# Scores in column groups and block transposes in the first layer of a two-layer attention kernel

## The chip, the core and the metric

The kernel runs on one core of a Trainium2 chip. A core has four compute engines with instruction streams of their own: TensorE (PE in the profile; its weight loads are shown as PEld), VectorE (DVE), ScalarE (ACT) and GpSimd (POOL). A fifth, SyncE (SP), issues most of the transfers. Each engine works through its stream in order, and the engines wait for each other by semaphores. The metric is the time of one execution on the device in microseconds; lower is better.

## The reference

The input x has 8 batches of 1024 tokens (64 positions l times 16 positions f) with 128 channels, in float32. The first layer is attention with 8 heads of width 128, whose scores are normalised twice, then a feed-forward layer with 512 hidden units and two layer norms:

```python
scores = jnp.einsum('bhlfc,bhmgc->bhlfmg', q, k) / jnp.sqrt(jnp.float32(c))
a = jax.nn.softmax(scores, axis=4)
a = jax.nn.softmax(a, axis=5)
z = jnp.einsum('bhlfmg,bhmgc->bhlfc', a, v)
...
z1 = _layer_norm(attn_out + x, ln1_g, ln1_b)
ffy = jax.nn.relu(z1 @ w1.T + b1) @ w2.T + b2
return _layer_norm(ffy + z1, ln2_g, ln2_b)
```

For one query, the 1024 scores are a grid of 64 positions m by 16 positions g. The first softmax runs over m, so it needs 16 sums of 64 exponentials each; the second runs over g, 64 sums of 16.

The second layer is additive attention within a batch, followed by a recurrence over the tokens with a sigmoid:

```python
scores = jnp.einsum('d,bijd->bij', v, jnp.tanh(Wi[:, None, :, :] + Wi[:, :, None, :]))
attn = jax.nn.softmax(scores, axis=-1)
C = jnp.einsum('bij,bjd->bid', attn, B)
```

That is a tanh for every pair of tokens and every channel. The scores are symmetric, so the kernel computes about half of the pairs.

## The kernel before

A program that runs when the data are within bounds (`fast_path`) does the work; a second, general program stands behind a branch and isn't entered here. The lines named below are those of the kernel before.

**First layer (`layer0`, once for each batch b).** The transposed input xT (channels on partitions, 1024 tokens along a row) is loaded by SP. For each head, `project` (L903) makes the query side u, with the product of the key and query weights folded into one matrix A, and `values` (L917) makes the values with the output weights folded in. For each of the 8 tiles of 128 queries:

- `scores` (L939): two products of 128 queries by 512 keys into the PSUM tile sc, so that a partition holds one query with all of its 1024 keys.
- the exponential on ACT, in place in PSUM (L942).
- `first_sums` (L946, DVE): 16 sums of 64; `first_inverse` (L949): 16 reciprocals; `divide` (L952): sc times these, into a half of the SBUF tile e.
- after two such tiles, a pair: one exponential over 2048 columns (L963, ACT), `second_sums` (L966) and `second_inverse` (L969) on DVE, and for each half `divide_again` on POOL (L980).
- the attention weights then have to stand with keys on partitions: for each half, eight transposes of 128x128 on PE (L853), four to a PSUM bank, and two copies of 128x512 out of PSUM into aT (L865 on DVE; for the first batch also L863 on ACT).
- `attend` (L994): eight products of 128x256, summed over the key tiles, and `gather` (L999 for head 0, L1001 else, DVE), which adds the result to zs.

After the heads follow the norm, the feed-forward part (`hidden`, `relu`, `outer`), which keeps its hidden units in an aT buffer, and the second norm.

**Second layer (`layer1`).** For each group of rows of the pair grid (`group`), either ACT computes tanh row by row with a bias (L1107), or POOL (L1117) or DVE (L1111, and a few L1117) adds the rows first and one wide tanh on ACT (L1165) follows. The rows stand in parts of a large SBUF tile th, which are given out and taken back (`Room`, `Span`). `times_v` (L1185) multiplies the rows by v on PE. Each of its products has 32 output partitions and uses one of four column groups of the array, into sa; a set of four fills all 128 partitions. After all rows of a tile come an exponential (L1281) and the attention of the second layer (L1314). At the end of the program, with all batches done, comes the recurrence (L1497, L1499).

**What sets the order.** All of this isn't issued as written. Every operation is registered with a `Plan` (`add`): the engines that it may run on and a cost in microseconds for each, the keys that it reads and writes, a priority and, if it needs one, a PSUM bank or a part of th. `Plan.emit` is a list scheduler: it keeps a clock for each engine, takes the engine that can start first and, among the operations that can start within 0.15 us of that, the one with the lowest priority number, and issues it. The tanh rows have several engines to choose from and go to the one that is free first in this reckoning. So a change of one operation's cost moves rows between ACT, POOL and DVE all through the program. PE operations have a mode, "full" or "groups" (column groups); a change of mode costs 0.1 us in the reckoning, and staying in the mode is preferred a little. The reckoning's costs are fixed numbers in the source; what the chip takes is another matter.

The first layer of batch b+1 runs beside the second layer of batch b (`pace` sets the priorities). The first layer of batch 0 runs with little beside it, and the second layer of batch 7 has nothing beside it at the end. `through_bank` registers a PE operation that takes one of the banks m0, m1 (for the first part of batch 0 also the two halves of sa) and the operation that empties it.

SBUF buffers that matter: two e pairs in `wx` (`es`, NE = 2), two aT buffers, th with 20 N columns (N = 1024). For batch 0 the values of the eight heads stand in th from 12 N on.

Of the kernel before, what the change touches and what calls it, by code (L numbers as in the profile page):

```python
# [10 lines left out]
AF = mybir.ActivationFunctionType  # L11
# [622 lines left out]
def fast_path(ctx: ExitStack, tc: tile.TileContext, a: dict, fits):  # L634
# [16 lines left out]
    NE = 2  # L651
# [33 lines left out]
    room = 20 * N  # L685
# [4 lines left out]
    aTs = ring("aT", 2, [P, NT, 2 * P])  # L690
    es = [wx[:, 4 + 2 * i : 6 + 2 * i, :] for i in range(NE)]
# [51 lines left out]


# [92 lines left out]
    count = {"aT": 0}  # L837

    def next_aT():
        count["aT"] += 1  # L840
        return (count["aT"] - 1) % 2

    def through_bank(pe, weight, r, evict, where, more, w, pri, choice=two):

        bank = Bank(*choice)
        n = len(plan.ops)
        add(("PE", weight), lambda _: pe(bank()), r=r, w=[("bank", n)], pri=pri, take=bank, wait=more + w)
        add(where, lambda e: evict(e, bank()), r=[("bank", n)] + more, w=w, pri=pri, give=bank)
# [23 lines left out]
    def layer0(b):  # L872
        alone = b == 0
        STRETCH = 0.95 if b < NB - 1 else 1.25
        xT, kx = xTs[b % 2], ("xT", b % 2)
        kz = ("zs",)
# [12 lines left out]
        for n_part, part in enumerate(parts):  # L889
# [3 lines left out]
            for h in range(H):  # L893
# [3 lines left out]
                if alone:  # L897
                    vp, kvp = th[:, (12 + h) * N : (13 + h) * N].rearrange("p (t c) -> p t c", c=C), ("vp0", h)
                for s in range(2) if part is None else (part,):
                    cols = slice(s * 512, (s + 1) * 512)  # L900

                    def project(bank, h=h, cols=cols):
                        nc.tensor.matmul(bank, A[:, h, :], xT[:, cols], start=True, stop=True)  # L903
# [20 lines left out]
                for qt in qts:  # L924
# [3 lines left out]
                    pair, q = (b * H * NT + i) // 2 % NE, qt % 2  # L928
# [3 lines left out]
                    r1, r2 = st[:, q, 0:G], st[:, :, G : G + M]  # L932
                    sc3 = sc.rearrange("p (m g) -> p m g", g=G)
                    e3 = e.rearrange("p (m g) -> p m g", g=G)

                    def scores(_, sc=sc, u=u, qt=qt):
                        for s in range(2):
                            cols = slice(s * 512, (s + 1) * 512)
                            nc.tensor.matmul(sc[:, cols], u[:, qt * P : (qt + 1) * P], xT[:, cols], start=True, stop=True)  # L939

                    add(("PE", 1.74), scores, r=[kx, ("u", h % 2, qt // 4)], w=[kc], pri=L0)
                    add(("ACT", 0.98), lambda _, sc=sc: nc.scalar.activation(sc, sc, AF.Exp, scale=SCALE),  # L942
                        r=[kc], w=[kc], pri=L0)

                    def first_sums(_, sc=sc, r1=r1):
# [642 lines left out]
```

## Time and profile before

| | us |
|---|---|
| median of 3 runs (5319.22 to 5320.98) | 5320.47 |
| the profiled execution | 5316.93 |
| its span, first to last instruction | 5315.0 |
| mean granted TensorE clock in it | 0.993 |

The profile gives for each engine the time in which it was busy, and for each group of instructions the busy time, the mean duration of one and the idle time of the engine in front of them with what ended it. The busy share by slices of a fortieth of the span, in tenths:

```profile
PE   8899999999999999999999999999999999986567
PEld 6555555555555555555555455555555455542125
DVE  7899999999999999999999999999999999988885
ACT  5489999999999999999999999999999999999994
POOL 2365779899998999999998999999899999987991
```

Three stages can be seen: the first three slices, some 400 us, in which the first layer of batch 0 runs and ACT is half idle; a long even part; and the last five slices, in which only the second layer of batch 7 and the recurrence are left. Most of the tanh work is in these groups:

```profile
L1117 POOL TENSOR_TENSOR th<-wiT 128x1024 f32<-128x1024 f32 (+59 forms) x2303 | 3345.5, 1487 | 215.2 <-PE sa L1185 196.0
L1165 ACT ACTIVATE th<-th 128x2634 f32<-128x2634 f32 (+53 forms) x997 | 2734.8, 2774 | 9.3 <-DVE th L1117 6.0
L1185 PE MATMUL sa<-th,vpat 128*32 128x512 f32 (+36 forms) x24576 | 2009.0, 459 | 202.2 <-ACT th L1165 186.9
L1111 DVE TENSOR_SCALAR_CACHE_REDUCE th<-wiT 128x344 f32<-128x344 f32 (+59 forms) x1930 | 1602.9, 867 | 68.6 <-PE sa L1185 65.8
L1107 ACT ACTIVATE th<-wiT 128x512 f32<-128x512 f32 (+62 forms) x1904 | 1369.8, 793 | 11.8 <-PE sa L1185 11.8
```

A line reads: source line, engine, operation, output and input tiles, form, count; then busy time in us and mean duration of one in ns; then the idle time before the group. A float32 product of PE appears as two records, so 24576 are 12288 products; a transpose is one record. ACT's tanh, 2734.8 and 1369.8 us, is more than three quarters of its time.

### The profile page before, as it was taken

Reading aid. Unit: us, or ns where it says so; the run is one execution under the profiler, and the core shown is the slowest. Engines: PE = TensorE matmul, PEld = TensorE weight load, DVE = VectorE, ACT = ScalarE, POOL = GpSimd, SP = SyncE. Lnnn points to the kernel's source line nnn. Section 1 sums busy time; section 2 is a strip of 40 time slices with the busy share of each in tenths; the row PEclk is TensorE's granted clock in tenths of the full one; section 3 lists DMA queues with packets and bytes.
Section 4 is the critical chain, followed back from the end, with each engine's and each line's share of the span. In section 5 each row is a group of like instructions: output and inputs, shape, how many; then the busy total and the mean of one; then the engine's idle time right before and its main releaser. Section 6 shows DMA issues by size and latency. Waiting matters only on the chain.

```text
span 5315.0 us, 98773 instructions
## 1 busy us (share of the span) xinstructions
PE 5007.1 (94%) x39173; PEld 2763.8 (52%) x39173; DVE 4884.6 (92%) x8676; ACT 5057.1 (95%) x4042; POOL 4522.8 (85%) x3113
## 2 busy tenths in 40 slices
PE   8899999999999999999999999999999999986567
PEld 6555555555555555555555455555555455542125
DVE  7899999999999999999999999999999999988885
ACT  5489999999999999999999999999999999999994
POOL 2365779899998999999998999999899999987991
PEclk9999999999999999999999999999999999999999
DMA  2000000000000000000000000000000000000001
GB/s 62 1 5 1 1 1 5 1 9 1 1 5 7 3 1 5 5 5 1 1 5 5 5 1 1 5 6 4 1 1 3 7 1 1 1 29 9 1 1 69
DMA packets 27335, 37.68 MB, mean 7 GB/s; under 512 B 2512, under 2 KB 19280, under 8 KB 26864
## 3 DMA queue, kind: packets, MB, share of 16 engines
q1 hardware_dynamic: 24832, 27.99, 1.6%
q8 instruction: 310, 5.08, 0.4%
q10 hardware_dynamic: 1872, 3.16, 0.2%
q14 instruction: 161, 1.32, 0.1%
q0 software_dynamic: 160, 0.13, 0.0%
HBM read 19.22 MB, written 12.06 MB: 6 GB/s over the span
## 4 chain that ended last, share of the span: by engine, by line
PE 67%; ACT 16%; DVE 10%; issue 6%; POOL 1%; DMA 0%; ACTq 0%; DVEq 0%; SPq 0%; POOLq 0%
PE sa L1185 25%; PE m L994 13%; PE sc L939 13%; ACT th L1165 9%; PE m L853 8%; ACT th L1107 4%; DVE th L1111 2%; PE m L1314 2%; PE m L917 2%; DVE stat_e L966 2%; PE m L903 1%; DVE stat_e L946 1%; ACT wx L963 1%; ACT sc L942 1%; DVE aT L865 1%
## 5 line engine op out<-in xcount | busy, mean ns | idle before, releaser
L1117 POOL TENSOR_TENSOR th<-wiT 128x1024 f32<-128x1024 f32 (+59 forms) x2303 | 3345.5, 1487 | 215.2 <-PE sa L1185 196.0
L1165 ACT ACTIVATE th<-th 128x2634 f32<-128x2634 f32 (+53 forms) x997 | 2734.8, 2774 | 9.3 <-DVE th L1117 6.0
L1185 PE MATMUL sa<-th,vpat 128*32 128x512 f32 (+36 forms) x24576 | 2009.0, 459 | 202.2 <-ACT th L1165 186.9
L1111 DVE TENSOR_SCALAR_CACHE_REDUCE th<-wiT 128x344 f32<-128x344 f32 (+59 forms) x1930 | 1602.9, 867 | 68.6 <-PE sa L1185 65.8
L1107 ACT ACTIVATE th<-wiT 128x512 f32<-128x512 f32 (+62 forms) x1904 | 1369.8, 793 | 11.8 <-PE sa L1185 11.8
L1185 PEld LDWEIGHTS sa<-th,vpat 128*32 128x32 f32 x24576 | 652.2, 110 | 1319.1 <-issue 842.2
L980 POOL TENSOR_TENSOR wx<-wx,stat_e 128x1024 f32<-128x1024 f32 x512 | 981.6, 1938 | 398.9 <-DVE stat_e L969 213.7
L939 PE MATMUL sc<-xT,wx 128*128 128x512 f32 x2048 | 983.5, 605 | 13.1 <-DVE wx L952 11.9
L994 PE MATMUL m<-aT,wx 128*128 128x256 f32 x3584 | 824.6, 384 | 7.2 <-DVE aT L865 7.2
L994 PEld LDWEIGHTS m<-aT,wx 128*128 128x128 f32 x3584 | 673.5, 191 | 187.8 <-issue 51.9
L865 DVE COPY aT<-m 128x512 f32<-128x512 f32 x940 | 616.6, 684 | 67.6 <-PE m L853 64.3
L946 DVE TENSOR_REDUCE stat_e<-sc 128x16 f32<-128x1024 f32 x512 | 613.5, 1204 | 38.9 <-ACT sc L942 37.7
L966 DVE TENSOR_REDUCE stat_e<-wx 128x128 f32<-128x2048 f32 x256 | 583.6, 2280 | 52.5 <-ACT wx L963 51.9
L952 DVE TENSOR_TENSOR wx<-sc,stat_e 128x1024 f32<-128x1024 f32 x512 | 619.9, 1214 | 3.2
L853 PEld LDWEIGHTS m<-ident,wx 128*128 128x128 f32 x3968 | 445.2, 141 | 309.4 <-issue 168.8
L942 ACT ACTIVATE sc<-sc 128x1024 f32<-128x1024 f32 x512 | 515.2, 1010 | 69.0 <-PE sc L939 52.8
L853 PE MATMUL m<-ident,wx 128*128 128x128 f32 x3968 | 558.6, 278 | 12.5 <-DVE aT L865 6.9
L939 PEld LDWEIGHTS sc<-xT,wx 128*128 128x128 f32 x2048 | 355.4, 191 | 385.8 <-issue 334.3
L963 ACT ACTIVATE wx<-wx 128x2048 f32<-128x2048 f32 x256 | 487.6, 1905 | 15.7 <-DVE wx L952 15.6
L969 DVE RECIPROCAL stat_e<-stat_e 128x128 f32<-128x128 f32 x256 | 240.9, 941 | 0.1
L1111 DVE DVE_READ_ACCUMULATOR th<-wiT 128x1 f32 x1930 | 160.8, 83 | 0.0
L917 PEld LDWEIGHTS m<-Wvo,xT 128*128 128x128 f32 x1080 | 133.9, 193 | 51.2 <-issue 25.0
(182 smaller groups left out, 2835.5 us busy)
## 6 DMA issues: line engine op xcount, KB each, us to landing
xT<-in_xt_dram SPq DMA_DIRECT2D x8, 512.0 KB, 3.6
th<-in_x_dram SPq DMA_DIRECT2D x8, 512.0 KB, 6.8
parked<-X SPq DMA_DIRECT2D x16, 256.0 KB, 2.3
xr<-parked SPq DMA_DIRECT2D x8, 512.0 KB, 8.1
parked_wx<-bT SPq DMA_DIRECT2D x14, 256.0 KB, 2.0
wx<-parked_wx SPq DMA_DIRECT2D x7, 512.0 KB, 3.2
out_dram<-ot ACTq DMA_DIRECT2D x8, 256.0 KB, 3.2
out_dram<-ot SPq DMA_DIRECT2D x8, 256.0 KB, 3.2
```

The source lines that it names most:

```text
L853: nc.tensor.transpose(bank[:, i * P : (i + 1) * P], s, ident)
L865: nc.vector.tensor_copy(dst, src)
L939: nc.tensor.matmul(sc[:, cols], u[:, qt * P : (qt + 1) * P], xT[:, cols], start=True, stop=True)
L946: nc.vector.tensor_reduce(r1, sc.rearrange("p (m g) -> p g m", g=G), AX.X, ALU.add)
L966: nc.vector.tensor_reduce(r2, e2.rearrange("p q (m g) -> p q m g", g=G), AX.X, ALU.add)
L980: nc.gpsimd.tensor_tensor(e3, e3, r2[:, q, :].unsqueeze(2).to_broadcast([P, M, G]), ALU.mult)
L994: nc.tensor.matmul(bank()[:, :256], vp[:, t, :], aT[:, t, :], start=t == 0, stop=t == NT - 1)
L1107: nc.scalar.activation(rows(c)[:, r, :], wiT[:, i0 + begin[c] :], AF.Tanh, bias=w_i(c, r))
L1111: nc.vector.tensor_scalar(rows(c)[:, r, :], wiT[:, i0 + begin[c] :], w_i(c, r), 0.0, ALU.add, ALU.add, accum_out=next_unused())
L1117: eng.tensor_tensor(rows(c), wiT[:, i0 + begin[c] :].unsqueeze(1).to_broadcast(shape), w_i(c).unsqueeze(2).to_broadcast(shape), ALU.add,)
L1165: nc.scalar.activation(slot()[:, a:z], slot()[:, a:z], AF.Tanh)
L1185: nc.tensor.matmul(sa[32 * c : 32 * c + 32, s:s1], vpat[:, 31 - r0 - r : 63 - r0 - r], rows(c)[:, r, s - at0 - begin[c] : s1 - at0 - begin ...
```

## The change

Layer 0's tiles of scores are laid out in another way, so that the block transpose of VectorE, which transposes 32x32 blocks, can take the place of the transposes on PE.

- xT holds the tokens in another order: the host puts token number 256 a + 32 b + r (a of 4, b of 8, r of 32) into column 128 b + 32 a + r, where before it stood in column 256 a + 32 b + r. `tokens` is the view of xT with the quarter a in front.
- `scores`: for a tile of 128 queries, 16 products instead of two. For each block s of 32 queries and each quarter a of the keys, the 32 queries are the stationary operand and the 256 keys of the quarter stream; the result goes to partitions 32 a to 32 a + 31, columns 256 s to 256 s + 255. A partition now holds one query's scores for a quarter of the keys, for each of four queries.
- `first_sums` gives 64 numbers for a partition (four queries by 16) that are sums over a quarter of the keys only. `totals`, four products of 32x64 on PE with the constant `same_row`, add the four quarters up and put the totals on all four partition groups, in a PSUM bank. `first_inverse` takes 64 reciprocals from the bank, and `divide` works as before on the new layout.
- After `divide_again`, `nc.vector.transpose` turns e in place, block by block of 32x32 (one instruction of 128x1024 for each half), in place of eight transposes on PE and two copies. `attend` streams the columns of e in runs of 32.
- The aT buffers are gone. There are three e pairs instead of two (NE = 3), handed out in turn, and the feed-forward part keeps its hidden units in an e pair. th grows by 448 columns. For batch 0 the values of heads 6 and 7 stand in buffers of X and B.
- `by_pe` is False throughout, so its branch isn't built. The costs given to the planner: totals 0.15, first_inverse 0.5 (before 0.2), the block transpose 1.17; the scores keep 1.74, in mode "groups".

```diff
-    NE = 2
+    NE = 3
...
-    room = 20 * N
+    room = 20*N+448
...
-    aTs = ring("aT", 2, [P, NT, 2 * P])
-    es = [wx[:, 4 + 2 * i : 6 + 2 * i, :] for i in range(NE)]
+    es = [wx[:, 4 + 2 * i : 6 + 2 * i, :] for i in range(2)] + ring("e", NE - 2, [P, 2, N])
...
+    same_row = tile_of(const, "same_row", [P, 32])
+    nc.vector.tensor_reduce(same_row, ident.rearrange("p (a r) -> p r a", a=4), AX.X, ALU.add)
...
+        tokens = xT.rearrange("p (b a r) -> p a b r", a=4, r=32)
...
-                    vp, kvp = th[:, (12 + h) * N : (13 + h) * N].rearrange("p (t c) -> p t c", c=C), ("vp0", h)
+                    at = 12 * N + h % 6 * N
+                    vp, kvp = th[:, at : at + N].rearrange("p (t c) -> p t c", c=C), ("vp0", h)
+                    if h >= 6:
+                        vp, kvp = (Xs[1], ("X", 1)) if h == 6 else (Bs[1][:, :, 0:C], ("B", 1))
...
-                        for s in range(2):
-                            cols = slice(s * 512, (s + 1) * 512)
-                            nc.tensor.matmul(sc[:, cols], u[:, qt * P : (qt + 1) * P], xT[:, cols], start=True, stop=True)
...
+                        for s in range(4):
+                            rows = slice(qt * P + 32 * s, qt * P + 32 * s + 32)
+                            for a in range(4):
+                                nc.tensor.matmul(
+                                    sc[32 * a : 32 * a + 32, 256 * s : 256 * s + 256], u[:, rows],
+                                    tokens[:, a], start=True, stop=True,
+                                )
...
+                        def first_sums(_, sc=sc, quarter=quarter):
+                            nc.vector.tensor_reduce(
+                                quarter.rearrange("p (s g) -> p s g", s=4),
+                                sc.rearrange("p (s m g) -> p s g m", s=4, g=G), AX.X, ALU.add,
+                            )
+
+                        def totals(bank, quarter=quarter):
+                            for a in range(4):
+                                nc.tensor.matmul(
+                                    bank[32 * a : 32 * a + 32, 0 : 4 * G], same_row, quarter, start=True, stop=True
+                                )
+
+                        def first_inverse(_, bank, quarter=quarter):
+                            nc.vector.reciprocal(quarter, bank[:, 0 : 4 * G])
+
+                        def divide(_, e=e, sc=sc, quarter=quarter):
+                            r = quarter.rearrange("p (s g) -> p s g", s=4).unsqueeze(2).to_broadcast([P, 4, G, G])
+                            nc.vector.tensor_tensor(quarters(e), quarters(sc), r, ALU.mult)
+
+                        add(("DVE", 1.15), first_sums, r=[kc], w=[k1], pri=L0)
+                        through_bank(totals, 0.15, [k1], first_inverse, ("DVE", 0.5), [], [k1], L0, banks, "groups")
+                        add(("DVE", 1.22), divide, r=[kc, k1], w=[ke], pri=L0)
...
-                        for s in range(2):
-                            through_bank(
-                                transposes([e[:, t * P : (t + 1) * P] for t in range(4 * s, 4 * s + 4)]), 0.52, [ke],
-                                copy(aT[:, 4 * s : 4 * s + 4, q * P : (q + 1) * P]), evict(0.68), [],
-                                [("aT", na, q, s)], L0, banks,
-                            )
+                        add(("DVE", 1.17), lambda _, e=e: nc.vector.transpose(e, e), r=[ke], w=[ke], pri=L0)
...
+                    keys = e2.rearrange("p q (s b r) -> p b (q s) r", s=4, r=32)
...
-                            nc.tensor.matmul(bank()[:, :256], vp[:, t, :], aT[:, t, :], start=t == 0, stop=t == NT - 1)
+                            nc.tensor.matmul(bank()[:, :256], vp[:, t, :], keys[:, t], start=t == 0, stop=t == NT - 1)
...
-        "xt": np.asarray(x).reshape(NB, N, C).transpose(0, 2, 1),
+        "xt": np.asarray(x).reshape(NB, 4, 8, 32, C).transpose(0, 4, 2, 1, 3).reshape(NB, C, N),
```

## The prediction

> **What bounds the kernel now.** I read the busy shares first, then the chain of waits, then four stretches cut at the ends of the 64th, 128th and last scores exponential (L942 at 392, 876 and 4687 us; a batch has 64 query tiles).
>
> ```profile
> PE 5007.1 (94%) x39173; PEld 2763.8 (52%) x39173; DVE 4884.6 (92%) x8676; ACT 5057.1 (95%) x4042; POOL 4522.8 (85%) x3113
> ...
> PE 67%; ACT 16%; DVE 10%; issue 6%; POOL 1%; DMA 0%; ACTq 0%; DVEq 0%; SPq 0%; POOLq 0%
> ...
> 0.00:392.00 392.00, 359.19 (x1729) 241.81 (x1730) 331.40 (x464) 241.72 (x372) 167.06 (x107) 1.00 0.08 22
> 392.00:876.00 484.00, 475.29 (x3379) 274.68 (x3377) 454.20 (x673) 470.03 (x540) 352.26 (x221) 1.00 0.01 2
> 876.00:4687.00 3811.00, 3749.47 (x29840) 2052.09 (x29838) 3593.12 (x6312) 3784.75 (x2746) 3554.17 (x2463) 1.00 0.01 4
> 4687.00:5315.00 628.00, 423.13 (x4231) 195.18 (x4229) 505.92 (x1229) 560.62 (x387) 449.33 (x324) 0.96 0.06 22
> ```
>
> Columns of the last four: length, then PE, weight loads, DVE, ACT, POOL. The chain says PE, 67%. But in the third stretch, 72% of the span, ACT is busy 3784.75 of 3811 us (99.3%): 26 us idle. PE is at 98.4%, DVE 94.3%. Two engines are full at once, so relieving PE alone can return no more there than ACT's 26 us plus whatever ACT work goes. In the first stretch ACT has 150 us idle and PE and DVE set the pace; in the last, PE has slack and ACT is full until the recurrence.
>
> The rows that the change touches:
>
> ```profile
> L952 DVE TENSOR_TENSOR wx<-sc,stat_e 128x1024 f32<-128x1024 f32 x512 | 619.9, 1214 | 3.2
> L865 DVE COPY aT<-m 128x512 f32<-128x512 f32 x940 | 616.6, 684 | 67.6 <-PE m L853 64.3
> L946 DVE TENSOR_REDUCE stat_e<-sc 128x16 f32<-128x1024 f32 x512 | 613.5, 1204 | 38.9 <-ACT sc L942 37.7
> ...
> L853 PE MATMUL m<-ident,wx 128*128 128x128 f32 x3968 | 558.6, 278 | 12.5 <-DVE aT L865 6.9 <-POOL wx L980 1.8 <-ACT aT L863 1.4
> ...
> L969 DVE RECIPROCAL stat_e<-stat_e 128x128 f32<-128x128 f32 x256 | 240.9, 941 | 0.1
> ...
> L949 DVE RECIPROCAL stat_e<-stat_e 128x16 f32<-128x16 f32 x512 | 117.8, 236 | 0.5
> ```
>
> **The change on PE.** Removed: 8 transposes for each of 512 tiles, 4096 at 558.6/3968 = 0.141 us: -577 us. The scores become 16 products of 32x256 instead of 2 of 128x512. The tanh products already run in this form:
>
> ```profile
> 3206.04 1.94 PE L1185 MATMUL sa<-th,vpat 128*32 128x256 f32 x32
> 3207.92 1.99 PE L939 MATMUL sc<-xT,wx 128*128 128x512 f32 x4
> 3209.74 1.04 PE L853 MATMUL m<-ident,wx 128*128 128x128 f32 x8
> ...
> 3118.93 1.10 PE L1185 MATMUL sa<-th,vpat 128*32 128x64 f32 x64
> 3119.96 1.12 PE L903 MATMUL m<-xT,A 128*128 128x512 f32 x2
> ```
>
> A matmul is two records, so the first line is exactly 16 products of 32x256: 1.88 us from start to start, against 1.82 for a tile's scores now (1.72 elsewhere). I take +0.11 x 512 = +56. The fourth line is 32 products of 64 columns in 1.03 us, 0.032 each; four for the totals are 0.13, x 512 = +66. PE: 5007 - 577 + 56 + 66 = 4552, 86%. That scores and attention now stream columns in runs of 32 is shown by no row; between 0 and 6% (a strided L946 against a dense L966: 1204 for 1024 against 2280 for 2048) of their 1925 us, 0 to +115. I take 0; PE is not the bound either way.
>
> L994 followed by L1185 takes 3.55 us from start to start (517.58 to 521.13), followed by full-size work 3.46 (255.99 to 259.45): 0.09 for a change of form, which lies inside the 1.88 above. Counted in the two instruction orders, changes between full size and column groups fall from 1730 to 1352, since the scores now stand beside the tanh products. [...]
>
> **DVE, per tile.** Two copies of 512 go (616.6/940 = 0.656 each). A 128x1024 block transpose comes; no row shows one. From below: the slope of L865, (684 - 281)/384 = 1.05 ns a column between 512 and 128 columns, gives 1.07; from above L1111 at 1024 columns, 1.27. I take 1.21, L952's, which is as wide. [...] The reciprocal grows from 16 to 64 columns: 0.236 + 48 x (0.941 - 0.236)/112 = 0.54, so +0.31 on 117.8/512 = 0.23; bounds 0 and +0.71. The sums keep their 1024 inputs and L946's price, the division L952's: 0 for both (if 64 outputs for 16 cost, L966 with 128 outputs says no).
>
> **What the planner moves.** The tanh rows go to whichever engine its list scheduler finds free, so the two instruction orders must be counted, stretch by stretch. Prices: an L1111 row with its accumulator read 0.29 + 1.037 us per 1000 columns (1272 + 83 at 1024, 490 + 83 at 270); L1107 0.216 + 0.838 and L1165 0.154 + 0.838 (slope from 3612 at 4096 and 1856 at 2000, the rest from their sums 1369.8 and 2734.8); an ACT copy of L863 0.57; an L1117 on DVE 101.7/80 = 1.27.
>
> To the 64th exponential, DVE: 58 copies fewer -38, 60 transposes +73, 63 reciprocals +20, 24 rows and 7474 columns more +15, one L1117 +1: +70, 401 us. ACT: 62 copies fewer -35, L1107 +116 rows, 25950 columns +47, L1165 +8, 21256 columns +19: 273.
> To the 128th, DVE: 119 copies -78, 64 transposes +77, reciprocals +20, 20 rows and 24083 columns +31, seven L1117 +9, norms -3: 510. ACT: -154 rows, -14961 columns -46; +32, +89134 columns +80; copies -3: 501.
> To the 512th, DVE: 772 copies -506, 386 transposes +467, 384 reciprocals +119, 98 rows and 90730 columns fewer -123, sixteen L1117 fewer -20, norms +3: 3533. ACT: +27261 columns of L1107 +23; -45 and -151606 of L1165 -134: 3674. POOL 69 fewer of L1117: about 3454.
> After it: ACT +5, DVE 0.
>
> So early work grows and the long stretch loses 111 us of ACT work, mostly the same work done sooner. Stretch one, cut again at 60 us: 60 us of start (DVE 27 busy), then 374 us of DVE, which ran at 305/332 = 92% with PE (308) at 93% beside it; PE now has room, so 96.5%: 388, in all 448 (+56). Two: 510 at 97%: 526 (+42). Three: ACT 3674 at 99.5%: 3692 (-119); DVE then stands at 95.7%. Four: 633 (+5). Sum 5299, against the span of 5315.0. The profiled run took 5316.93, 1.9 more than its span, and the median is 3.5 above it: forecast 5304, own range 5287 to 5320.
>
> What hides what: the round trip DVE to PE to DVE for the totals is hidden by other DVE work standing between sums and reciprocal (never fewer than one instruction in the new order, mostly two to six). Behind a late reciprocal DVE's in-order queue stops; next late are the division, ACT's second exponential and POOL's L980, which waits for L969 already (213.7 us). The new wait for a bank takes the place of four bank fills per pair. The third e pair and the other placing of the first batch's values add no instruction; a spare buffer can save a wait, 0 taken. The block order of xT is the host's; its eight loads keep their 512 KB, their queue and place.
>
> **Rivals.**
> 1. The round trip is not hidden, and DVE becomes the bound. DVE waits 0.07 us a copy for PE now (64.3/940), and 0.16 a gather (39.9 us on 256 gathers, L999 and L1001). At 0.16 a totals product, with its other waits kept: stretch one 60 + 374 + 27 + 10 = 471; two 510 + 30 + 10 = 550; three 3533 + 218 - 64 + 61 = 3748; four 633: 5402, and 5407 as a median. It decides once DVE's share of the third stretch stays under 95.3% (3533/3708, the length that brings the sum back to 5315). For it: in none of the four stretches does DVE pass 94.3%. Against: its waits were on a PE at 98%.
> 2. An exchange: idle times stay, the early loss cancels the gain: 462 + 525 + 3700 + 633 = 5320, median 5325: no change. For it: ACT was full before. Against: idle in stretch one came while PE was full.
> 3. PE was the true bound, as the chain says: every stretch closes to its fullest engine at 99% (60 + 374/0.99 = 438; 510/0.99 = 515; ACT 3674/0.999 = 3677; the last 633 less 8 = 625): 5255, median 5260. Against: ACT's 26 us.
> That the scores in column groups do not overlap is excluded by the 3206.04 line.
>
> **How the numbers follow.** Forecast 0.42, rival 1 0.30, rival 2 0.15, rival 3 0.13. A measurement of this kernel tells about 0.2%, 11 us, from no change. Faster: most of the forecast and rival 3, 0.46; within: rival 2 and the forecast's upper edge, 0.16; slower: rival 1 and the rest, 0.38. The range, 5250 to 5395, reaches past rival 3 and nearly to rival 1; the transpose at 1.07 (-72 us of DVE) and at 1.27 (+31) lie in it.
>
> **What would show it.** PE near 86%; scores near 1.9 us a tile; transposes near 1.21; reciprocals near 0.54; the 64th exponential at about 448, the 128th at 974, the last at 4666; ACT over 99% between the last two. Wrong if DVE waits for the totals by more than 0.1 us a tile, if a transpose takes 1.4, or if ACT's idle time between the last two passes 45 us.

## The result, and the profile after

| | before | after |
|---|---|---|
| median, us (4 runs each, same chip) | 5319.88 | 5369.98 |
| lowest to highest | 5319.22 to 5320.98 | 5367.01 to 5372.08 |
| span of the profiled execution | 5315.0 | 5364.7 |
| mean granted TensorE clock | 0.993 | 0.974 |

The ratio is 1.0093, with a 95% interval of 1.0077 to 1.0109: the changed kernel is 50 us slower. The forecast was 5304, 16 us faster.

The busy times and the chain of waits of the changed kernel, from its page:

```profile
PE 4753.6 (89%) x53509; PEld 2598.9 (48%) x53509; DVE 4941.9 (92%) x8132; ACT 5017.7 (94%) x3947; POOL 4578.8 (85%) x3162
...
ACT 40%; PE 34%; DVE 15%; issue 9%; POOL 1%; DMA 0%; ACTq 0%; SPq 0%; DVEq 0%; POOLq 0%
```

PE did get 253 us lighter and the chain left it (67% before, 34% now). ACT has 39 us less to do than before. What grew is the time in which ACT does nothing: 5315.0 - 5057.1 = 258 us before, 5364.7 - 5017.7 = 347 us now. That account, ACT's busy time plus its idle time, is used below; it doesn't say what causes the idle time.

The same kernel cut at the 64th, 128th and 512th scores exponential. Columns: length, then PE, weight loads, DVE, ACT and POOL busy, the granted clock, DMA share and rate:

```profile
0.00:473.60 473.60, 381.40 (x3919) 237.67 (x3920) 398.24 (x520) 274.04 (x436) 192.23 (x127) 0.93 0.07 19
473.60:1001.80 528.20, 486.61 (x5643) 269.46 (x5645) 506.36 (x673) 511.45 (x419) 475.25 (x315) 0.98 0.01 2
1001.80:4734.90 3733.10, 3458.51 (x39772) 1899.36 (x39766) 3529.13 (x5701) 3669.62 (x2700) 3439.24 (x2388) 0.99 0.01 4
4734.90:5364.70 629.80, 427.09 (x4197) 192.43 (x4185) 508.17 (x1241) 562.61 (x396) 472.03 (x334) 0.94 0.06 21
```

Beside the forecast (the cuts of the kernel before, at its exact markers, are 392.8, 884.1 and 4690.2):

| stretch | before | forecast | after | ACT busy, forecast / after | DVE busy, forecast / after |
|---|---|---|---|---|---|
| 1 | 392.8 | 448 | 473.6 | 273 / 274.0 | 401 / 398.2 |
| 2 | 491.3 | 526 | 528.2 | 501 / 511.5 | 510 / 506.4 |
| 3 | 3806.1 | 3692 | 3733.1 | 3674 / 3669.6 | 3533 / 3529.1 |
| 4 | 624.8 | 633 | 629.8 | 566 / 562.6 | 506 / 508.2 |

The work on ACT and DVE was forecast within about 2% in each stretch. Two lengths miss: the first by 26 us, the third by 41. In both, ACT waits longer than the forecast allowed.

The waits of ACT, after and then before: engine, line, what it waited for, us in total, times, longest.

```profile
ACT sc L956 <- PE sc L948: 131.6, 50, 10.8
ACT wx L1024 <- DVE wx L1013: 61.1, 12, 28.8
```

```profile
ACT sc L942 <- PE sc L939: 52.8, 49, 6.3
...
ACT wx L963 <- DVE wx L952: 15.6, 12, 3.4
```

The first exponential waits for scores (+79 us), the second for the division (+45 us). And DVE itself, did it wait for the totals? The groups of the changed kernel that answer to the forecast's prices:

```profile
L1042 DVE STREAM_TRANSPOSE wx<-wx 128x1024 f32<-128x1024 f32 x342 | 416.7, 1225 | 3.9 <-POOL wx L1039 3.8
...
L1009 DVE RECIPROCAL stat_e<-m 128x64 f32<-128x64 f32 x492 | 261.7, 534 | 22.1 <-PE m L1004 20.9
...
L1004 PE MATMUL m<-stat_e,same_row 128*32 128x64 f32 x3936 | 149.5, 226 | 57.7 <-DVE stat_e L997 43.5 <-DVE stat_e L1009 4.9 <-DVE wx L867 2.2
```

It hardly did: 20.9 us over the program, 0.04 us a tile. The delay is there all the same, and is seen when each reciprocal is paired with the sums it belongs to in the timeline:

| mean, us | before, stretch 1 / 2 / 3 | after | totals left out (`no_totals`, below) |
|---|---|---|---|
| end of the sums to start of the reciprocal | 0.9 / 1.2 / 1.4 | 3.3 / 4.5 / 6.3 | 1.5 / 1.6 / 1.5 |
| start of the sums to end of the division | 4.7 / 5.2 / 5.5 | 7.6 / 8.8 / 10.6 | 6.1 / 6.4 / 6.9 |

DVE fills the gap with other work, as forecast; but the tile's scores stay in sc until the division has read them, and there are two sc tiles. In stretch one a tile now holds its sc for about 2.0 us of products, 1.0 of exponential and 7.6 up to the end of the division, 10.6 us, or 5.3 us a tile with two of them, out of (473.6 - 60)/64 = 6.5. Before it was 1.9 + 1.0 + 4.7, or 3.8 of 5.2. The waits that lie between add to both.

Where it is worst can be seen in one place. ACT around 1060 us (start, length, and in brackets the idle time in front):

```profile
1042.39 1.01 ACT L956 ACTIVATE sc<-sc 128x1024 f32<-128x1024 f32 x1 [8.80 <-PE sc L948]
...
1046.43 1.01 ACT L956 ACTIVATE sc<-sc 128x1024 f32<-128x1024 f32 x1
1076.23 1.91 ACT L1024 ACTIVATE wx<-wx 128x2048 f32<-128x2048 f32 x1 [28.79 <-DVE wx L1013]
...
1089.38 5.30 ACT L1164 ACTIVATE th<-wiT 128x1024 f32<-128x1024 f32 x5 [8.37 <-DVE wiT L1289]
```

From 1033.6 to 1089.4, 56 us, ACT is idle for 46 in these three waits, and has no tanh row in its stream. The kernel before has only one wait above 3 us in all of its third stretch (3.81). The longest of the three is traced here; that the other two come of the totals as well isn't shown. DVE and then PE in the same place:

```profile
1050.86 1.16 DVE L997 TENSOR_REDUCE stat_e<-sc 128x64 f32<-128x1024 f32 x1
...
1052.59 1.21 DVE L997 TENSOR_REDUCE stat_e<-sc 128x64 f32<-128x1024 f32 x1
...
1072.67 0.55 DVE L1009 RECIPROCAL stat_e<-m 128x64 f32<-128x64 f32 x1
```

```profile
1058.57 2.08 PE L1098 MATMUL m<-zs,w_sb 128*128 128x512 f32 x2
...
1066.44 1.06 PE L1120 MATMUL m<-w_sb,wx 128*128 128x128 f32 x8
1067.34 3.62 PE L1050 MATMUL m<-e,wx 128*128 128x256 f32 x16
1071.53 0.32 PE L1004 MATMUL m<-stat_e,same_row 128*32 128x64 f32 x8 [0.58 <-DVE zs L1056]
```

The sums of the two tiles are done at 1052.0 and 1053.8; the first totals, 0.3 us of work, run at 1071.5. In PE's in-order stream they stand behind the feed-forward part of the batch (L1098, L1120) and an `attend` (L1050), which take the same two banks and themselves wait for DVE. Both sc tiles wait for totals, so no new scores come. Before, sums, reciprocal and division were three DVE instructions, and nothing on PE could stand between them.

### The profile page after: what moved, and what is told of

The parts are those of the page before. It is cut to its first block, busy times and chain, and to the rows that moved or that the text cites. A ratio compares the mean times of both kernels' runs of the same rounds, so it can differ in the third digit from the quotient of the medians.

```text
span 5364.7 us, 126448 instructions
## 1 busy us (share of the span) xinstructions
PE 4753.6 (89%) x53509; PEld 2598.9 (48%) x53509; DVE 4941.9 (92%) x8132; ACT 5017.7 (94%) x3947; POOL 4578.8 (85%) x3162
## 4 chain that ended last, share of the span: by engine, by line
ACT 40%; PE 34%; DVE 15%; issue 9%; POOL 1%; DMA 0%; ACTq 0%; SPq 0%; DVEq 0%; POOLq 0%
ACT th L1222 21%; PE sa L1242 12%; ACT th L1164 11%; PE m L1050 7%; PE sc L948 7%; ACT sc L956 4%; DVE th L1168 3%; ACT wx L1024 2%; DVE stat_e L1027 2%; DVE stat_e L997 2%; DVE wx L1013 1%; PE m L1371 1%; ACT e L1024 1%; PE m L923 1%; POOL th L1174 1%
## 5 line engine op out<-in xcount | busy, mean ns | idle before, releaser
L1174 POOL TENSOR_TENSOR th<-wiT 128x240 f32<-128x240 f32 (+53 forms) x2352 | 3383.9, 1475 | 141.3 <-PE sa L1242 104.8
L1222 ACT ACTIVATE th<-th 128x3194 f32<-128x3194 f32 (+52 forms) x995 | 2700.2, 2748 | 4.9 <-DVE th L1168 3.5
L1242 PE MATMUL sa<-th,vpat 128*32 128x512 f32 (+32 forms) x24576 | 2098.1, 464 | 376.6 <-ACT th L1222 337.5
L1168 DVE TENSOR_SCALAR_CACHE_REDUCE th<-wiT 128x684 f32<-128x684 f32 (+59 forms) x1887 | 1529.4, 851 | 62.7 <-PE sa L1242 59.3
L1164 ACT ACTIVATE th<-wiT 128x504 f32<-128x504 f32 (+56 forms) x1876 | 1389.3, 811 | 16.8 <-DVE wiT L1289 13.2
L948 PE MATMUL sc<-xT,wx 128*32 128x256 f32 x16384 | 1002.9, 386 | 54.6 <-DVE wx L1013 34.1
L948 PEld LDWEIGHTS sc<-xT,wx 128*32 128x32 f32 x16384 | 512.6, 111 | 463.1 <-issue 98.4
L997 DVE TENSOR_REDUCE stat_e<-sc 128x64 f32<-128x1024 f32 x512 | 613.1, 1200 | 44.8 <-ACT sc L956 43.6
L1050 PE MATMUL m<-wx 128*128 128x256 f32 x2400 | 564.6, 389 | 9.7 <-DVE wx L1042 5.8
L1050 PEld LDWEIGHTS m<-wx 128*128 128x128 f32 x2400 | 449.4, 192 | 140.3 <-issue 33.7
L1042 DVE STREAM_TRANSPOSE wx<-wx 128x1024 f32<-128x1024 f32 x342 | 416.7, 1225 | 3.9 <-POOL wx L1039 3.8
L1050 PE MATMUL m<-e,wx 128*128 128x256 f32 x1184 | 280.8, 391 | 12.0 <-DVE e L1042 7.1
L1009 DVE RECIPROCAL stat_e<-m 128x64 f32<-128x64 f32 x492 | 261.7, 534 | 22.1 <-PE m L1004 20.9
L1050 PEld LDWEIGHTS m<-e,wx 128*128 128x128 f32 x1184 | 223.3, 194 | 73.1 <-issue 13.0
```

The source lines that it names most:

```text
L948: nc.tensor.matmul(sc[32 * a : 32 * a + 32, 256 * s : 256 * s + 256], u[:, rows], tokens[:, a], start=True, stop=True,)
L997: nc.vector.tensor_reduce(quarter.rearrange("p (s g) -> p s g", s=4), sc.rearrange("p (s m g) -> p s g m", s=4, g=G), AX.X, ALU.add,)
L1050: nc.tensor.matmul(bank()[:, :256], vp[:, t, :], keys[:, t], start=t == 0, stop=t == NT - 1)
L1164: nc.scalar.activation(rows(c)[:, r, :], wiT[:, i0 + begin[c] :], AF.Tanh, bias=w_i(c, r))
L1168: nc.vector.tensor_scalar(rows(c)[:, r, :], wiT[:, i0 + begin[c] :], w_i(c, r), 0.0, ALU.add, ALU.add, accum_out=next_unused())
L1174: eng.tensor_tensor(rows(c), wiT[:, i0 + begin[c] :].unsqueeze(1).to_broadcast(shape), w_i(c).unsqueeze(2).to_broadcast(shape), ALU.add,)
```

## The experiments

All ratios are to the kernel before on the same chip. "Theory D" in some expectations: the loss is the work given to VectorE. Where a run is compared with the changed kernel, that is 5370.

### Is it the wait for the totals?

`no_totals` takes the reciprocals of the sums over a quarter of the keys:

```diff
-through_bank(totals, 0.15, [k1], first_inverse, ("DVE", 0.5), [], [k1], L0, banks, "groups")
+add(("DVE", 0.5), lambda e, f=first_inverse, quarter=quarter: f(e, quarter), r=[k1], w=[k1], pri=L0)
```

> Leaves out the adding up of the four quarters: the reciprocal reads VectorE's own 64 sums from SBUF, so that the four small products and the detour VectorE, TensorE, VectorE are gone; VectorE's instructions stay the same. Theory W (the first stretch is long because VectorE has 92 us of transposes and longer reciprocals there, which ScalarE and TensorE cannot take): the 64th exponential moves by less than 15 us from 474, the time stays within 20 us of 5370. Theory R (the detour is not hidden: it lengthens the time for which a tile holds one of the two scores buffers, and VectorE idles behind it): the 64th exponential comes by 440 or earlier and the time falls to 5310 or less.

`totals_unread` issues the four products too, into a bank that nothing reads, and takes the reciprocals as above:

```diff
+unread = Bank(*banks)
+add(("PE", 0.15), lambda _, totals=totals, unread=unread: totals(unread()), r=[k1], pri=L0, mode="groups",
+    take=unread, give=unread)
```

> Keeps the four small products of each tile on TensorE, into a bank as before, but nobody reads them: the reciprocal reads VectorE's own sums (the adding up of the quarters is left out). TensorE's work is that of the changed kernel, only the wait is gone. Theory R: the same gain as without the products, within 15 us. If instead the products themselves or their changes of form cost (TensorE's work and its bank), the time stays above 5345. Theory W: within 20 us of 5370 here as well.

Measured: 5341.3 (1.0032, 1.0016 to 1.0047) and 5331.5 (1.0022, 1.0012 to 1.0032), 29 and 38 us below the changed kernel. Neither theory is met in full: the times lie between the 5350 of theory W and the 5310 of theory R. The second run is within 15 us of the first, as theory R asked, so it isn't the products' time on PE that costs. The 46 us at 1060 are gone in both: no wait above 3 us between 880 and 1180. A loss of 17 and 12 us against the kernel before stays by these ratios (22 and 12 by the medians).

Both runs also have another order of the work, since the planner no longer reckons with the wait, and the lengths of the stretches show it:

| stretch | forecast | after | `no_totals` | `totals_unread` |
|---|---|---|---|---|
| 1 | 448 | 473.6 | 444.2 | 445.1 |
| 2 | 526 | 528.2 | 449.2 | 448.9 |
| 3 | 3692 | 3733.1 | 3824.6 | 3809.0 |
| 4 | 633 | 629.8 | 622.8 | 626.8 |

The first two stretches are 108 us shorter together, and the third is 91 and 76 us longer: ACT work that was done early now comes later (702 us of it in the first two stretches of `no_totals`, for 786). ACT's wait for scores, in the two runs:

```profile
ACT sc L956 <- PE sc L948: 110.3, 38, 11.1
```

```profile
ACT sc L957 <- PE sc L949: 93.8, 39, 11.1
```

Of the 79 us that this wait had grown by, 21 and 38 go with the wait for the totals. The rest isn't explained by it.

### The transposes alone

`tr_alone` is the kernel before with the block transposes of `e` in place of the PE transposes and copies; scores, sums and reciprocals are the old ones.

```diff
-through_bank(transposes([e[:, t * P : (t + 1) * P] for t in range(4 * s, 4 * s + 4)]), 0.52, [ke],
-    copy(aT[:, 4 * s : 4 * s + 4, q * P : (q + 1) * P]), evict(0.68), [], [("aT", na, q, s)], L0, banks)
+add(("DVE", 1.17), lambda _, e=e: nc.vector.transpose(e, e), r=[ke], w=[ke], pri=L0)
```

> The kernel before with one part of the change alone: VectorE's block transpose in place and attention from e, instead of TensorE's transposes and the copies; scores, 16 sums and 16 reciprocals as before, no totals, two e pairs. (Left out: keys and queries are not brought across the 32x32 blocks.) Theory W (VectorE's own work in batch 0 sets the loss): the 64th exponential comes at 430 or later, since 73 us of transposes replace 38 us of copies there, and the time is 5315 to 5345. Theory R (the detour for the totals sets it): the 64th exponential comes at 420 or earlier and the time is 5260 to 5300, below the kernel before.

Measured: 5275.7 (0.9914, 0.9897 to 0.9931). The time is that of theory R, but the 64th exponential comes at 430.8, where theory W had it. ACT waits for scores here too, 30 us longer than in the kernel before, with neither the totals nor the new scores. So the block transposes, or the order that comes with them, make it wait as well; which of the two was not tried:

```profile
ACT sc L942 <- PE sc L939: 83.0, 44, 7.7
```

The exchange on its own is worth 46 us, though the weights of a pair then don't stand where `attend` needs them; the new layout that puts them there costs 94 more in the changed kernel.

### Which batches lose?

`bype_first` builds, for batch 0 only, the branch that the change left out (16 products on PE for the first sums, 16 reciprocals, 16 small products to spread them). `old_first` does batch 0 as in the kernel before: two full products, 16 sums and reciprocals on DVE, PE transposes and copies.

```diff
-by_pe = False
+by_pe = alone
```

> For the tiles of batch 0 alone the first sums are made by TensorE too (16 products of 32x64 into a bank, a short reduction of 64 columns on VectorE, then 16 small products that spread the reciprocals): VectorE loses about 1 us of each of the 64 tiles, TensorE gains as much, and there are two detours through TensorE instead of one. Theory W: the first stretch shortens by 45 to 75 us from 474, the time falls to 5300 to 5335. Theory R: the second detour makes the first stretch longer or leaves it within 15 us of 474.

```diff
-add(("PE", 1.74), scores, r=[kx, ("u", h % 2, qt // 4)], w=[kc], pri=L0, mode="groups")
+add(("PE", 1.74), plain_scores if alone else scores, r=[kx, ("u", h % 2, qt // 4)], w=[kc], pri=L0,
+    mode="full" if alone else "groups")
...
+if not alone:
+    add(("DVE", 1.17), lambda _, e=e: nc.vector.transpose(e, e), r=[ke], w=[ke], pri=L0)
+    continue
```

> Batch 0 in the layout of before (two products for the scores, 16 sums, transposes on TensorE with copies that ScalarE shares), batches 1 to 7 as changed. Both theories: the 64th exponential comes back to 392 within 15 us. If the loss is only that of the first stretch, the time is 5290 to 5320, under the kernel before; if the later stretches give it back (ScalarE, full there, gets the work that was done early in the changed kernel), it is 5320 to 5350.

Measured: 5354.3 (1.0062, 1.0042 to 1.0082) and 5292.4 (0.9951, 0.9934 to 0.9967). Batch 0 in the new form costs 78 us, more than the whole loss, and without it the change gains 26. But the length of stretch one is not what counts: `bype_first` ends it at 411.7, 62 us earlier than the changed kernel, and ends the program only 16 earlier. ACT's idle time tells the two apart: 337 us in `bype_first`, 251 in `old_first`, of it 185 and 137 in stretch one (200 in the changed kernel). `bype_first` met theory W with its stretch one, not with its time; `old_first` met the first of its two ranges.

`old_first` keeps the totals in batches 1 to 7. Their reciprocals stand 4.8 and 6.3 us behind the sums in stretches two and three, as late as in the changed kernel, and yet it is 26 us faster than the kernel before. So the delay doesn't cost wherever it stands: where the runs show a cost of it, it is in batch 0 and where batch 0 ends.

### Is it VectorE's work?

`recip16` takes 16 reciprocals in place of 64 and divides all four queries by them; the planner is told 0.2. `recip16_notot` leaves out the totals as well.

```diff
-nc.vector.reciprocal(quarter, bank[:, 0 : 4 * G])
+nc.vector.reciprocal(quarter[:, 0:G], bank[:, 0:G])
...
-through_bank(totals, 0.15, [k1], first_inverse, ("DVE", 0.5), [], [k1], L0, banks, "groups")
+through_bank(totals, 0.15, [k1], first_inverse, ("DVE", 0.2), [], [k1], L0, banks, "groups")
```

> The changed kernel with 16 reciprocals a tile in place of 64 (0.24 us by the 16-column rows of the other runs, against 0.534; cost to the planner 0.2 for 0.5); all four queries of a partition are divided by the first one's sums, so the other three queries' own sums are left out. The way through PE and the order of the work stay. Theory D (what the new layout costs beside the wait for the totals is work given to VectorE: 0.30 us x 512 = 153 us that it lacks for its tanh rows): 5335 or below, ScalarE idle near 310 us in place of 347. Rival G (the cost lies in the scores by column groups and the lower granted clock of TensorE, and VectorE's extra work is nothing): 5355 to 5380.

> As the kernel with 16 reciprocals, and the totals on PE are left out as well: the reciprocals are taken of the sums over a quarter of the keys. What is left of the new layout is the scores by column groups and the block transpose; the VectorE work is that of the kernel with the transposes alone (5276). Theory D: the two costs add, 5265 to 5300. Rival G: 5310 to 5345, that is near 5341 of the kernel without the totals, since the scores by column groups are still there.

Measured: 5302.1 (0.9966, 0.9954 to 0.9979) and 5313.0 (0.9983, 0.9973 to 0.9992). The first met theory D with 68 us. The second is in rival G's range, though 28 us below the 5341 that it was to be near: with short reciprocals, leaving the totals out gave nothing (11 us slower), so the two costs don't add. That raised the question whether the work or the order of the work had made the 68 us, since the planner's order had changed with the told 0.2. Three runs complete the square of order and work: `recip16_order` (16 reciprocals, told 0.5), `after_told02` (64 reciprocals, told 0.2), and `recip_twice` (the 64 reciprocals issued twice, told 0.5).

> The kernel with 16 reciprocals a tile (the other three queries' own sums left out), but with the planner told 0.5 for them as in the changed kernel, so that every engine gets the order of the changed kernel: only the duration of 512 instructions differs, 0.24 for 0.53 us. Theory D1 (the time of these instructions on VectorE is itself in the way, by waits that follow on it): 5295 to 5330. Rival O (the 68 us that the shorter reciprocals gave came from another order of the work): 5350 to 5372.

> The changed kernel, everything computed, with each of the 64-column reciprocals issued twice, in the order of the changed kernel: 512 x 0.53 = 273 us more on VectorE. Theory D1: if 0.30 us less gives some 40 us or more, 0.53 more costs at least 70: 5440 or above, and up to 5640 if VectorE never has spare time. Rival O: under 5410.

> The changed kernel, everything computed, 64 reciprocals of 0.53 us a tile, but with the planner told 0.2 for them in place of 0.5: the work of the changed kernel in the order (and with the allotment of rows) of the run with 16 reciprocals. In the changed kernel's own order 153 us less of VectorE gave nothing. If the time follows the order (the rows that the planner gives VectorE, which has time to spare), 5300 to 5325; if the 64 reciprocals are too much for an order that has 123 more rows on VectorE, VectorE becomes the bound: 5350 to 5400.

| median, us | order for 0.5 | order for 0.2 |
|---|---|---|
| 16 reciprocals | 5368.2 | 5302.1 |
| 64 reciprocals | 5370.0 | 5332.9 |
| 64, twice | 5495.9 | |

(Ratios to before: 1.0091 [1.0074, 1.0108] and 1.0024 [1.0014, 1.0033] for the two new ones, 1.0330 [1.0313, 1.0347] for the doubled one.) In the changed kernel's own order, 136 us less busy time on DVE (4806.2 for 4941.9) give nothing. Why, its page and its timeline say. The busy times and chain of `recip16_order`, then its ACT at the place shown above:

```profile
PE 4758.1 (89%) x53509; PEld 2604.9 (49%) x53509; DVE 4806.2 (90%) x8132; ACT 5016.9 (94%) x3947; POOL 4580.5 (85%) x3162
...
ACT 42%; PE 35%; DVE 12%; issue 9%; POOL 2%; DMA 0%; ACTq 0%; POOLq 0%; SPq 0%; DVEq 0%
```

```profile
1073.56 1.91 ACT L1026 ACTIVATE wx<-wx 128x2048 f32<-128x2048 f32 x1 [28.26 <-DVE wx L1013]
```

The hole is still there, 28.26 us for 28.79: it is made by where the totals stand on PE, not by DVE's speed. Stretch one is only 3 us shorter (470.6). So `recip16_order` met rival O. Doubling instead of shortening does make DVE the bound, as the chain of `recip_twice` shows:

```profile
DVE 60%; PE 20%; ACT 10%; issue 8%; POOL 1%; DMA 0%; SPq 0%; ACTq 0%; DVEq 0%; POOLq 0%
```

So DVE had slack in the changed kernel, but less than the 248 us of busy time added here (4941.9 to 5189.6, for a program 126 us longer): rival 1's bound was near and not reached. And the order for 0.2 alone, with exactly the changed kernel's instructions to do, is worth 37 of the 68 us, although 0.2 is the wrong price and 0.5 the right one (0.534 measured). Its 5332.9 lies between the two ranges. The wait for the totals is in it (3.3, 4.0 and 6.3 us between sums and reciprocal), so a mere change of order gave as much as taking the wait out. Two things differ in it. The planner gives DVE 123 more tanh rows; the group in the changed kernel and in `after_told02`:

```profile
L1168 DVE TENSOR_SCALAR_CACHE_REDUCE th<-wiT 128x684 f32<-128x684 f32 (+59 forms) x1887 | 1529.4, 851 | 62.7 <-PE sa L1242 59.3 <-issue 2.3
```

```profile
L1168 DVE TENSOR_SCALAR_CACHE_REDUCE th<-wiT 128x776 f32<-128x776 f32 (+56 forms) x2010 | 1636.4, 856 | 51.2 <-PE sa L1242 48.2 <-issue 1.7 <-ACT th L1222 0.3
```

And around 1050 us its ACT waits only 3.3, 4.3, 4.9 and 6.7 us, 19 in place of 46. ACT's busy time falls by 9 us, its idle time by 22. With the full reciprocals that order has DVE at 5036 us and in the chain with 37%; shortening them there gives the other 31 us.

### How much is the luck of one order?

`LEAD`, the lead of the first layer's priorities, moved by 0.01 issues the same work in another order:

```diff
-LEAD, DOWN, SOON, LATE = 0.35, 0.06, 0.5, -0.3
+LEAD, DOWN, SOON, LATE = 0.36, 0.06, 0.5, -0.3
```

> The kernel before with the lead of the first layer's priorities at 0.36 instead of 0.35, nothing else: how far the list scheduler's order alone moves the time. If orders are alike (structure theory): within 10 us of 5319. If the order before was a lucky one (luck theory): 5345 or more, as much as the whole change cost.

> The changed kernel with the lead at 0.36 instead of 0.35, nothing else. Structure theory: within 10 us of 5370, the 64th exponential at 474 within 5. Luck theory: 20 us or more off in either direction.

> The kernel before with the lead at 0.34 (0.36 gave 5383, 0.35 is 5320). If 5320 is what its work takes in most orders: 5310 to 5340. If 0.35 was a lucky order: 5350 or above, and the loss of the change is then within what an order is worth.

> The changed kernel with the lead at 0.34 in place of 0.35 (0.36 gave 5377): another order of the same work. If the change's loss against the kernel before is more than the luck of two orders, both kernels at 0.34 differ as at 0.35, by 30 to 70 us: 5350 to 5400. If it is luck, this comes out at or below the kernel before with the same edit.

| median, us | 0.34 | 0.35 | 0.36 |
|---|---|---|---|
| before | 5329.1 | 5319.9 | 5383.2 |
| after | 5376.4 | 5370.0 | 5377.5 |
| batch 0 old, other first sums on PE (below) | 5274.5 | 5273.5 | 5319.0 |

The intervals are about 0.17% to either side or less. The change loses 47 and 50 us in two of the three and is 6 us ahead in the third, so an order is worth as much as the change. The hole of the changed kernel stands in all three of its orders (28.8, 28.8 and 28.1 us, ending near 1077). But these orders are alike up to there: by the traces, the streams of ACT and DVE part from those of the changed kernel at 1391 us (0.34) and at 1000 us (0.36). In the order for 0.2 the hole isn't there. So it belongs to one way of issuing batch 0, and what the lead shows of luck lies behind stretch one.

### A version that beats both

`bype_half` builds the first sums on PE for every other pair of tiles. `old_first_all` takes batch 0 in the old form and builds all other first sums on PE.

```diff
-by_pe = False
+by_pe = i // 2 % 2 == 0
```

> Everything is computed. For every other pair of tiles the branch that the change leaves unbuilt is built: 16 products on PE make the first sums (VectorE reduces only 64 columns of a bank), 16 reciprocals, and 16 small products spread them. By the rows of the run with this branch in the first batch that takes 1.20 + 0.53 - 0.20 - 0.24 = 1.30 us off VectorE and adds some 0.8 us to PE on each of 256 tiles: VectorE -333 us, PE +205 us (4754 to about 4960). Theory D: 5260 to 5330, at or below the kernel before. Rival G (VectorE's work is not what costs, PE's detours and clock are): 5365 to 5410, since PE gets two detours a tile for one.

```diff
 # on top of old_first
-by_pe = False
+by_pe = not alone
```

> Everything is computed. Batch 0 as in the kernel before (two full products, transposes on PE, copies), batches 1 to 7 with the block transposes and with all first sums on PE (VectorE -1.30 us on 448 tiles, PE +0.8). Theory D: below the 5292 of the run that has only batch 0 in the old form, 5240 to 5290. If PE becomes the bound (4736 + 448 x 0.8 = 5094 us busy, 96% of 5290, more than the 94% of the kernel before): 5300 to 5340. Rival G: 5310 or above.

> The same version with the lead at 0.34. As for 0.36: 5260 to 5310 if it is better by its work, 5320 or above if the order was a lucky one.

> The version with batch 0 in the old form and all other first sums on PE (5273.5), with the lead of the first layer's priorities at 0.36 in place of 0.35: the same work in another order. If that version is better by its work, this stays below the kernel before, 5260 to 5310; if it was a lucky order, 5320 or above, as the kernel before became 5383 by the same edit.

Measured: `bype_half` 5294.4 (0.9950, 0.9933 to 0.9966); `old_first_all` 5273.5 (0.9918, 0.9901 to 0.9934), 46 us faster than the kernel before and 96 faster than the changed one; with the lead at 0.34 0.9915 (0.9898 to 0.9931), at 0.36 0.9998 (0.9989 to 1.0008), where the kernel before with the same edit is at 1.0118. At each lead it is the fastest of the three, by 46 to 64 us against the kernel before. At 0.36 its 5319.0 lies between the two ranges named; the other three met theory D, or "better by its work". The page of `old_first_all`:

```profile
PE 4909.6 (93%) x76805; PEld 2993.4 (57%) x76805; DVE 4743.9 (90%) x9037; ACT 4984.3 (95%) x3708; POOL 4480.6 (85%) x3084
...
PE 63%; ACT 17%; DVE 12%; issue 5%; POOL 1%; DMA 0%; SPq 0%; ACTq 0%; DVEq 0%; POOLq 0%
```

It gives PE two detours a tile where the changed kernel has one, and yet is faster. Its first exponential goes from PSUM into SBUF (e), which frees sc at once in batches 1 to 7, so no wait for PE holds a score tile there (ACT waits 42 us for scores, 35 of them in batch 0, for 132 in the changed kernel); it also takes 198 us off DVE, and batch 0 doesn't use the detours at all. Which of these is worth how much was not tried one by one. `bype_first` has the two together in batch 0: ACT's wait for scores in stretch one is 14 us there, for 104 in the changed kernel.

## Why the prediction was wrong, point by point

- **The work.** Right where it set the lengths: transposes 1.22 us (forecast 1.21), 64 reciprocals 0.534 (0.54), scores 1002.9/512 = 1.96 a tile (near 1.9), and the rows that the planner moved. For the transpose, the estimate from below, by the slope of L865's copies, was 1.07 us; the measured row (L1042, 1.225) is 14% longer.
- **PE.** Forecast 4552, measured 4753.6. The totals took 0.30 us a tile for 0.13, so the price read inside a run of 32 such products didn't hold for four that stand alone (+90); the tanh products took 2098.1 for 2009.0 (+89); `attend` +32, scores -37, the rest +27. Two changes of form at each of 512 scores and 512 totals, at the 0.09 us between the forecast's two L994 lines, would make it 4736, by an estimate. That sum is near, and half of the charge fits: it puts 92 us on the totals, which came out 90 over, and 92 on the scores, which came out under. Whether the totals' excess comes of such changes no run here shows. PE had room for all of it: 89%.
- **The step that failed** is "What hides what": "the round trip DVE to PE to DVE for the totals is hidden by other DVE work standing between sums and reciprocal", costed at nothing. It was hidden from DVE, with 0.04 us of waiting a tile. It was not hidden from what the tile holds meanwhile: 2.4 to 4.9 us more between sums and reciprocal, and the two sc tiles kept longer. Stretch one ends at 474 and 468 in the two orders with this wait and 64 reciprocals (told 0.5 and 0.2), at 444 and 445 in the two without it; with 16 reciprocals told 0.2, at 452 with it and 437 without. And one place of the totals in PE's stream makes the longest wait of ACT, 28.8 us. The forecast named the division and ACT as next late, and looked only for what would make DVE wait; it did not ask where the totals stand in PE's stream. How much of the 50 us this wait is stays open: leaving it out gave back 29 and 38 us, but in other orders of the work, and another order with the wait left in gave back 37.
- **The efficiencies** failed as well. Stretch one was worked out from DVE's work at 96.5% after its first 60 us, because PE would have room. DVE ran at 371.35 of 413.6, 90%, and without the totals at 354.77 of 384.2, 92%, as in the kernel before: PE's room didn't help (+26 us). That `no_totals` ends the stretch near the forecast's 448 is in part luck, since the planner gives DVE less to do there, 381 us for 401. Nor does DVE's work alone set this length: 14 us less of it in the same order (`recip16_order`) made it 3 us shorter. ACT at 99.5% in stretch three: 98.3%, and 46 of its 63 idle us are the waits around 1060 (+41 us). The condition "ACT's idle time between the last two passes 45 us" for being wrong was met; "DVE waits for the totals by more than 0.1 us a tile" was not, though the totals are what it meant. The cuts at 876 and 4687 stood 8 and 3 us before the ends that they were named for; this moves time from one stretch to the next and leaves the sum.
- **Rival 1** had the place, the round trip, and almost the length of stretch one (471 for 473.6) but the wrong bound: DVE was not it. The chain shows ACT and PE, and 136 us less DVE work in the same order changed nothing. Its 5407 is what DVE as the bound would have meant; `recip_twice` shows that state.
- **Rival 2** (idle times stay) was wrong too: idle time of ACT rose by 89 us. Its 525 for stretch two also follows from neither engine's idle time (510 + 30 for DVE, 501 + 14 for ACT). **Rival 3** had the right sign for the exchange alone (5276 for `tr_alone`; it said 5260), and failed with the layout, which made the time 94 us longer.
- **What stays open.** With the wait removed, 12 to 22 us of loss are left, and how the layout's 94 us divide isn't settled: the wait, the longer reciprocal and the order overlap (`recip16_notot` is slower than `recip16`), and any single comparison of two orders carries an uncertainty up to the 62 us by which 0.01 of lead moved the kernel before. That time is lost to the wait is seen in stretch one, in every pair of runs with and without it, and in the 28.8 us of one order; for the program as a whole it is argued, since the order changed each time. Why batch 0 costs more than the other seven together was shown as a size, not traced to one wait.

## What to carry to other kernels

A detour over another engine is not hidden because the engine that asked has other work: ask what the data holds until the answer is back (here one of two PSUM tiles), and what stands in the other engine's queue in front of the small operation. Where a planner allots work, an edit's cost is the change of the whole order and allotment; shift an unrelated priority a little in both versions before believing a difference of 1%. Try a change part by part: the same exchange of the transposes, with the old form kept in the first batch and the score tiles freed early, gained 46 to 64 us in three orders.

## What the runs showed of the hardware

From 60 us to the 64th exponential the granted TensorE clock is by and large lower in the versions in which PE is less busy. Before, and then after (PE busy in the second column, clock third from the end):

```profile
60.00:392.80 332.80, 308.33 (x1474) 200.50 (x1473) 305.45 (x425) 217.14 (x316) 156.60 (x91) 0.99 0.00 1
```

```profile
60.00:473.60 413.60, 329.96 (x3470) 196.60 (x3470) 371.35 (x482) 247.52 (x377) 182.66 (x112) 0.92 0.01 2
```

PE busy at 93% has 0.99, at 80% 0.92; `recip_twice` there has 77% and 0.90, `old_first_all` 91% and 1.00; not strictly so, since `recip16` has 82% and 0.96, `totals_unread` 83% and 0.93. The busy share alone doesn't give the clock: in the last stretch PE is busy at 67 to 68% in the kernels before and after, with 0.96 and 0.94. What share of the time this costs was not measured. A reciprocal's time follows its columns: 0.236 us for 16, 0.534 for 64, 0.94 for 128. A 128x1024 block transpose in place took 1.225 us.
